# Draining GpSimd's indirect transfers in pairs, in a planned two-layer kernel on one core

## The chip, the core and the metric

The kernel runs on one core of one Trainium2 chip. A core has five engines that each work through a queue of their own in order: TensorE (PE) multiplies matrices, VectorE (DVE) and ScalarE (ACT) work on tiles element by element, GpSimd (POOL) does slower element work and issues transfers whose addresses come from data, and SyncE (SP) issues the other transfers. Semaphores order the queues among each other. The metric is the device time of one execution in microseconds; less is better.

## The reference

Eight sequences of 1024 tokens with 128 channels pass through two layers, each a mixer and a feed-forward network with a layer norm before it and a residual around it. Cut to what matters here:

```
x = L0_attn_x                                     # 8 x 1024 x 128
x = x + L0_attn(layernorm(x))                     # decayed linear attention, a scan over tokens
x = x + L0_ffn(layernorm(x))                      # 8 experts, top 2, hidden width 352
x = x + L1_attn(layernorm(x))                     # conv, gate, selective scan with 16 states
x = x + L1_ffn(layernorm(x))                      # 8 experts, top 2, width 128, and 2 shared ones

# a routed network, for each token:
scores = softmax(xn @ Wg.T); w, idx = top_k(scores, 2)
y = sum over e in idx of w_e * (silu(xn @ W1[e].T) * (xn @ W3[e].T)) @ W2[e].T
```

## The kernel before

Each sequence is one job of four stages, `l0_attn`, `l0_ffn`, `l1_attn` and `l1_ffn`, on tiles of 128 x 1024. The eight jobs overlap: at most five hold an x tile at once, and instructions of several stand mixed in each engine's queue.

The order of the work is fixed when the program is built. Every step is recorded with `op` (line 106): its engine, a planner's duration in us, what it reads and writes, and `land`, the time a transfer takes to land after its issue. `Schedule.run` (line 144) is a list scheduler. It keeps a clock for each engine, takes the step with the earliest start, and among steps that can start within `NEAR` of each other takes the one that is due first. `AHEAD` and `STAY` hold back ScalarE steps that would load another activation table. The due times come from `TIMES` (line 63), a row for each sequence: when its x is loaded, and for each of the four stages the due times of its first, second and last part. `START` (line 74) has the due times of the copies of the weights and of the zeroing of the scratch arrays. Nothing of this runs on the chip: there each engine takes its instructions in the order written, and waits on semaphores alone.

The two routed networks use scratch arrays in device memory. `dispatch` (line 767) normalizes x, routes, works out a row number `at` for each of 2 x 1024 token copies, so that each block of 128 rows belongs to one expert, copies the normalized rows on GpSimd (line 792) to add the second copy's weight, and then puts the rows into `xd` with sixteen indirect transfers of 128 rows from GpSimd (line 813). `block_pair` (line 844) loads two blocks of `xd` with SyncE into `xg` and transposes them on TensorE; `fetch` loads the block's expert weights; the result is weighted on ScalarE (line 879) and stored in `yd`. `combine` (line 825) gets the rows back with sixteen indirect transfers on GpSimd (line 832), eight for each of two tiles `g`, and after each eight adds the tile to x on GpSimd (line 842). The next stage's layer norm reads x on VectorE (line 478).

The last sequence's `l1_ffn` is computed densely, without routing, so there are 15 dispatches and 15 combines, with 240 puts and 240 gets.

GpSimd has one more task, in `l1_attn`: for each of the 16 states VectorE scans (line 1025) into one of four `st` tiles, multiplies it, and for all states but the first GpSimd adds the product to y (line 1035). These adds, the puts, the gets and the adds to x share GpSimd's queue.

Of the kernel before, what the change touches and what calls it, by code (L numbers as in the profile page):

```python
# [18 lines left out]
P = 128  # L19
T = 1024  # L20
NC = T // P
# [19 lines left out]
NST = 16  # L41
# [9 lines left out]

PE, DVE, ACT, POOL, SP = ENGINES = "PE", "DVE", "ACT", "POOL", "SP"
HOP = 0.1
NEAR = 0.141
TABLE = 1.3
AHEAD = 44.7
STAY = 675.97


FREE = "wide", "acc", "row", "tile64", "xg", "xgT", "h", "ysb"  # L60


TIMES = (
    (0.00, (266.32, 1847.59, 2307.10), (3760.69, 4450.59, 4867.29), (4934.72, 4936.07, 5074.67), (5113.40, 5139.16, 5310.29)),
    (3.56, (3273.27, 4241.54, 4793.32), (4824.85, 4945.95, 4955.40), (5096.98, 5279.14, 5301.11), (5442.87, 5510.48, 5668.30)),
    (28.59, (3893.45, 4841.22, 4949.32), (4949.33, 5011.59, 5200.87), (5345.49, 5546.91, 5863.91), (5880.85, 5880.86, 6091.76)),
    (119.24, (4827.78, 4983.48, 5011.45), (5165.22, 5267.56, 5525.66), (5818.86, 6051.79, 6090.06), (6103.71, 6186.21, 6934.85)),
    (389.34, (5188.77, 5392.69, 5604.20), (5636.54, 5802.06, 6027.87), (6100.87, 6527.36, 6941.79), (7032.13, 7164.73, 7772.04)),
    (504.89, (5416.94, 5669.81, 5921.96), (5948.26, 6168.24, 6435.93), (6843.69, 7190.63, 7603.76), (7857.58, 7879.15, 8348.80)),
    (728.44, (6007.28, 6161.19, 6660.77), (6720.53, 6797.55, 7398.14), (7815.93, 8928.93, 9119.46), (9483.85, 9651.23, 10294.32)),  # L70
    (977.51, (6389.60, 6695.97, 7179.18), (7248.10, 7635.87, 7924.00), (8346.44, 9746.01, 10107.23), (10122.54, 10230.87, 10523.57)),
)

START = 65.94, 32.93, 130.54, -2689.22, 619.92, 9.07


class Buf:
# [133 lines left out]
def preln_two_layer_kernel(ctx: ExitStack, tc: tile.TileContext, a: dict, out: bass.AP):  # L211
    nc = tc.nc
# [149 lines left out]
    def pick(r):  # L362

        return eye3b[:, r : r + 1].to_broadcast([TERMS * NBC, P])
# [45 lines left out]
        return t.unsqueeze(2).to_broadcast([P, NC, n])  # L410

    def dve_us(n, two=True):
        return 0.1 + n * (1.04e-3 if two else 0.62e-3)

    def act_us(n):
        return 0.14 + n * 0.86e-3

    def tt(out_, in0, in1, alu, n, r, w, eng=DVE):
        e = nc.vector if eng == DVE else nc.gpsimd
        us = dve_us(n) if eng == DVE else 0.1 + n * 2.35e-3  # L420
        op(eng, us, lambda: e.tensor_tensor(out_(), in0(), in1(), alu), r, w)  # L421

    def stt(out_, in0, scalar, in1, op0, op1, n, r, w):
# [30 lines left out]
            hold=hold,  # L454
        )

    def mm_cols(dst, m, lhsT, rhs, r, us=1.0):


        def fn():  # L460
            for s in range(T // HALF):
                nc.tensor.matmul(  # L462
                    dst.f[:m, ts(s, HALF)], lhsT(), rhs()[:, ts(s, HALF)], start=True, stop=True
                )

        op(PE, 2 * us, fn, r, [dst])

    def normal(x):

        xw, stats = Buf("xw"), Buf("stats")  # L470
        total, dev, var = Buf("row"), Buf("row"), Buf("row")
        st = lambda i: stats.f.rearrange("p (c s) -> p c s", s=6)[:, :, i]
        row = lambda b: lambda: b.f


        def moments():
            for c in range(NC):
                nc.vector.bn_stats(stats.f[:, 6 * c : 6 * c + 6], x3(x)[:, c, :])  # L478

        op(DVE, NC * 0.2, moments, [x], [stats])  # L480
        tt(row(dev), lambda: st(1), lambda: st(4), ALU.subtract, NC, [stats], [dev])
        tt(row(var), lambda: st(2), lambda: st(5), ALU.add, NC, [stats], [var])
        stt(row(dev), row(dev), 0.25, row(dev), ALU.mult, ALU.mult, NC, [dev], [dev])
        stt(row(var), row(var), 1.0 / P, row(dev), ALU.mult, ALU.add, NC, [var, dev], [var])

        act(row(var), row(var), AF.Ln, NC, [var], [var], "exp", bias=eps)
        tt(row(total), lambda: st(1), lambda: st(4), ALU.add, NC, [stats], [total])
        rstd, shift = Buf("row"), Buf("row")
        act(row(rstd), row(var), AF.Exp, NC, [var], [rstd], "exp", scale=-0.5)
        stt(row(shift), row(total), -0.5, row(rstd), ALU.mult, ALU.mult, NC, [total, rstd], [shift])  # L490

        def scale():
            for c in range(NC):
                nc.scalar.activation(  # L494
                    v3(xw, NC, XW)[:, c, :P], x3(x)[:, c, :], AF.Identity,
                    scale=rstd.f[:, c : c + 1], bias=shift.f[:, c : c + 1],
                )

        op(ACT, NC * 0.26, scale, [x, rstd, shift], [xw])
        return xw  # L500

    def turned(xw, tag):

        pt, xnT = Buf("wide"), Buf(tag)

        def fn():
            for c in range(NC):
                nc.tensor.transpose(pt.f[:, ts(c, P)], v3(xw, NC, XW)[:, c, :P], ident)

        op(PE, 1.6, fn, [xw], [pt])  # L510
        copy_act(lambda: xnT.f, lambda: pt.f, T, [pt], [xnT])
        return xnT

    def router(xnT, wgT, bias):
# [9 lines left out]
                    v3(pg, NC, NE)[:, c, :], xnT.f[:, ts(c, P)], wgT, start=True, stop=True  # L524
                )

        op(PE, 1.9, logits, [xnT], [pg])
        mx, p, tot = Buf("row"), Buf("tile64"), Buf("row")
        reduce(lambda: mx.f, t3(pg), ALU.max, n, [pg], [mx])
        tt(t3(p), t3(pg), lambda: per_token(mx.f, NE), ALU.subtract, n, [pg, mx], [p])  # L530
# [108 lines left out]
    def to_tokens(parts, consume, r=()):  # L639

        for q in range(NC // 4):
            po = Buf("acc")

            def fn(po=po, q=q):
                for i in range(4):
                    for j, (h, w) in enumerate(parts):
                        nc.tensor.matmul(  # L647
                            v3(po, 4, P)[:, i, :],
                            h.f[:, ts(4 * q + i, P)],
                            w(),  # L650
                            start=(j == 0),
                            stop=(j == len(parts) - 1),
                        )

            op(PE, 4 * len(parts) * 0.26, fn, [*(h for h, _ in parts), *r], [po])
            consume(4 * q, po)

    def add_to(x):
# [63 lines left out]
    def l0_attn(x, b):  # L722
# [23 lines left out]
        for f0 in range(0, EDIM, FGRP):  # L746
            parts = []
            for f in range(f0, f0 + FGRP):
                kv = Buf("kv")
                load(  # L750
                    lambda kv=kv: kv.f,
                    lambda f=f: heads_to_channels(vr.f[:, f, :]), 512, [vr], [kv],
                )
                tt(lambda kv=kv: kv.f, lambda: kT.f, lambda kv=kv: kv.f, ALU.mult, T, [kT, kv], [kv])
                op(
                    DVE, 2.25,
                    lambda kv=kv: nc.vector.tensor_tensor_scan(  # L757
                        kv.f, lam.f, kv.f, 0.0, ALU.mult, ALU.add
                    ),
                    [lam, kv], [kv],  # L760
                )
                tt(lambda kv=kv: kv.f, lambda: qT.f, lambda kv=kv: kv.f, ALU.mult, T, [qT, kv], [kv])
                parts.append((kv, lambda f=f: o_rep[:, f, :]))
                yield
            to_tokens(parts, add_to(x))

    def dispatch(x, i, tag, wgT, bias):
# [40 lines left out]
        views = dram_disjoint_views(xd[i], TOPK * NC)  # L808
        for k in range(TOPK):
            for c in range(NC):  # L810
                op(
                    POOL, 1.3,
                    lambda k=k, c=c: nc.gpsimd.indirect_dma_start(  # L813
                        out=views[k * NC + c],
                        out_offset=bass.IndirectOffsetOnAxis(
                            ap=v3(at, TOPK, NC)[:, k, c : c + 1].bitcast(I32), axis=0
                        ),
                        in_=r3[k]()[:, c, :],
                        in_offset=None,
                    ),  # L820
                    [rows[k], at], [(xd_b[i], (k, c))], land=2.8,
                )
        return at, expert, xnT

    def combine(x, i, at):

        for k in range(TOPK):
            g = Buf("tmp")
            for c in range(NC):
                op(  # L830
                    POOL, 1.28,
                    lambda k=k, c=c, g=g: nc.gpsimd.indirect_dma_start(  # L832
                        out=v3(g, NC, P)[:, c, :],
                        out_offset=None,
                        in_=yd[i],
                        in_offset=bass.IndirectOffsetOnAxis(
                            ap=v3(at, TOPK, NC)[:, k, c : c + 1].bitcast(I32), axis=0
                        ),
                    ),
                    [yd_b[i], at], [(g, c)], land=2.5,  # L840
                )
            tt(lambda: x3(x), lambda: x3(x), lambda g=g: v3(g, NC, P), ALU.add, T, [x, g], [x], POOL)

    def block_pair(i, xdb):
# [10 lines left out]
            for q in range(n):  # L855
                nc.tensor.transpose(pt.f[:, ts(q, P)], v3(xg, 2, XW)[:, q, :P], ident)

        op(PE, 0.05 + 0.18 * n, turn, [xg], [pt])
        copy_act(lambda: xgT.f[:, : n * P], lambda: pt.f[:, : n * P], n * P, [pt], [xgT])
        return n, xg, xgT, ysb  # L860

# [30 lines left out]
    def l0_ffn(x, b):  # L892
# [4 lines left out]
        def second(i, we, h, xg, ysb):  # L897
# [8 lines left out]
                        start=(j == 0), stop=(j == 2),  # L906
                    )

            op(PE, 0.85, fn, [h, we], [py])
            weigh(py, xg, ysb, i, 0)  # L910
            if i % 2 or i == NBLK - 1:
                keep(ysb, ydb, i - i % 2, i % 2 + 1)
# [2 lines left out]
        for i in range(NBLK):  # L915
# [11 lines left out]
                            start=True, stop=True,  # L927
                        )

            op(PE, 1.6, first, [we, xgT], [p13])  # L930
            act(lambda h=h: h.f, lambda p13=p13: p13.f[:, : 3 * P], AF.Silu, 3 * P, [p13], [h], "silu")
            tt(
                lambda h=h: h.f, lambda h=h: h.f, lambda p13=p13: p13.f[:, HALF : HALF + 3 * P],
# [11 lines left out]
    def l1_attn(x, b):  # L945
# [67 lines left out]
        for n in range(NST):  # L1013
# [1 line left out]
            act(  # L1015
                lambda da=da: da.f, dtf, AF.Exp, T, [dt], [da], "exp", scale=a_mat[:, n : n + 1]
            )
            mm_cols(pb, P, lambda n=n: pick(n), b3, [bc3], us=0.3)
            tt(
                lambda pb=pb: pb.f, lambda: dtx.f, lambda pb=pb: pb.f, ALU.mult, T,  # L1020
                [dtx, pb], [pb],
            )
            op(
                DVE, 2.25,
                lambda st=st, da=da, pb=pb: nc.vector.tensor_tensor_scan(  # L1025
                    st.f, da.f, pb.f, 0.0, ALU.mult, ALU.add
                ),
                [da, pb], [st],
            )
            mm_cols(pcc, P, lambda n=n: pick(NST + n), b3, [bc3], us=0.3)  # L1030
            stf = lambda st=st: st.f
            hc, hcf = (st, stf) if n else (y, yf)
            tt(hcf, stf, lambda pcc=pcc: pcc.f, ALU.mult, T, [st, pcc], [hc])
# [48 lines left out]
    def l1_ffn(x, b):  # L1082
# [22 lines left out]
        def second(i, n, w, h, xg, ysb):  # L1105
# [6 lines left out]
                        start=True, stop=True,  # L1112
                    )

            op(PE, 0.38 * n, fn, [h, *w], [py])
            for q in range(n):
                weigh(py, xg, ysb, i + q, q * P)
            keep(ysb, ydb, i, n)
# [2 lines left out]
        for i in range(0, NBLK, 2):  # L1121
# [9 lines left out]
                            start=True, stop=True,  # L1131
                        )

            op(PE, 0.7 * n, first, [xgT, *w], [p13])
            hf = lambda h=h, n=n: h.f[:, : n * P]
            act(hf, lambda p13=p13, n=n: p13.f[:, : n * P], AF.Silu, n * P, [p13], [h], "silu")
            tt(
# [108 lines left out]
```

## Time and profile before

| | |
|---|---|
| median of 3 runs | 2038.16 us (2036.46 to 2038.98) |
| the profiled execution | 2030.27 us |
| its span, first to last instruction | 2028.5 us |
| instructions in the span | 24,884 |
| mean granted TensorE clock | 0.819 of full |
| indirect transfers on GpSimd | 480, 31.61 MB on the software queue |
| transfers issued by SyncE | 247.81 MB on queue q1 |
| activation table loads on ScalarE | 198, 1.283 us each |

The profiled execution is one execution with the hardware profiler on; its own time is 7.9 us under the median of the three timed runs. The span lies 1.8 us under its time. Shares of busy time are averages over the span. An instruction of GpSimd that issues a transfer is shown as DMA_INDIRECT with the time that GpSimd spent on it; the transfer itself is seen in the packets of the software queue.

### The profile page before, as it was taken

To read this page: it belongs to the slowest core of one execution; us is meant where nothing else is said; L and a number is where in the kernel's file an instruction comes from. 1 tells how busy PE (TensorE), PEld (TensorE's weight loads), DVE (VectorE), ACT (ScalarE), POOL (GpSimd) and SP (SyncE) were. 2 spreads that over 40 slices of the span, in tenths; PEclk is the share of its full clock that TensorE was granted. 3 is DMA by queue.
4 is the path that set the end of the run, shared out by engine and by line. 5 is a ranking of instruction groups with operands and counts; after the bars stand their busy time and mean duration, and the time that the engine had idled before them with its cause. 6 is when DMAs were issued, how large, how long until landed. Compare 5 with 4: busy or idle time off the path is not lost. (4 is left out here: it accounts for less than half of the span.)

```text
span 2028.5 us, 24884 instructions
## 1 busy us (share of the span) xinstructions
PE 1385.9 (68%) x7693; PEld 1062.5 (52%) x7693; DVE 1441.4 (71%) x2117; ACT 998.4 (49%) x1657; POOL 895.1 (44%) x662
## 2 busy tenths in 40 slices
PE   2448786867666778567856676956765767656587
PEld 0336775646453665455654565645754555433365
DVE  1775656877566978499865977799756626888955
ACT  3213332753745575345746456663744366583441
POOL 0030312255346632666354574276455633736613
PEclk9759797888977889768887888977886788786679
DMA  5847575344336465444435664634543555332231
GB/s 131 199 123 201 178 215 152 113 147 150 115 106 186 120 182 163 105 139 130 131 121 154 188 180 126 192 106 140 166 143 116 160 160 166 84 99 63 75 89 56
DMA packets 215740, 282.54 MB, mean 139 GB/s; under 512 B 24248, under 2 KB 173112, under 8 KB 215608
## 3 DMA queue, kind: packets, MB, share of 16 engines
q1 hardware_dynamic: 194504, 247.81, 42.2%
q0 software_dynamic: 15360, 31.61, 5.2%
q10 hardware_dynamic: 5744, 1.54, 0.4%
q8 instruction: 61, 1.00, 0.2%
q14 instruction: 71, 0.58, 0.1%
HBM read 223.62 MB, written 63.15 MB: 141 GB/s over the span
## 5 line engine op out<-in xcount | busy, mean ns | idle before, releaser
L421 POOL TENSOR_TENSOR y<-y,st 128x1024 f32<-128x1024 f32 x120 | 291.7, 2430 | 299.1 <-DVE st L421 284.2
L925 PE MATMUL wide<-xgT,we 128*128 128x128 f32 x2208 | 323.9, 305 | 56.1 <-ACT xgT L449 15.2
L832 POOL DMA_INDIRECT tmp<-yd,at x240 | 260.8, 1087 | 216.8 <-issue 93.6
L925 PEld LDWEIGHTS wide<-xgT,we 128*128 128x128 f32 x2208 | 305.1, 219 | 82.6 <-ACT xgT L449 19.1
L1025 DVE TENSOR_TENSOR_SCAN st<-da,wide 128x1024 f32<-128x1024 f32 x128 | 292.4, 2284 | 8.2
L462 PE MATMUL wide<-term,eye3b 96*128 96x512 bf16 x512 | 178.3, 448 | 131.6 <-DVE st L1025 83.2
L904 PE MATMUL acc<-we,h 128*128 128x128 f32 x1104 | 182.9, 309 | 122.8 <-DVE h L421 63.7
L393 ACT ACT_TABLE_LOAD x198 | 254.0, 1283 | 18.0 <-DMA wgT<-in_gate_wT_dram 14.5
L904 PEld LDWEIGHTS acc<-we,h 128*128 128x128 f32 x1104 | 159.5, 216 | 154.6 <-issue 57.0
L813 POOL DMA_INDIRECT xd<-xw,at x120 | 123.9, 1033 | 247.2 <-DVE at L634 183.4
L879 ACT ACTIVATE ysb<-acc,xg 128x128 f32<-128x128 f32 x345 | 115.9, 363 | 218.2 <-PE acc L904 65.5
L421 DVE TENSOR_TENSOR h<-h,wide 128x384 f32<-128x384 f32 x184 | 99.7, 547 | 155.5 <-ACT h L446 103.1
L446 ACT ACTIVATE h<-wide 128x384 f32<-128x384 f32 x184 | 89.5, 489 | 242.7 <-PE wide L925 176.5
L421 DVE TENSOR_TENSOR wide<-dtx,wide 128x1024 f32<-128x1024 f32 x128 | 156.6, 1224 | 60.0 <-PE wide L462 27.5
L446 ACT ACTIVATE da<-dt,a_mat 128x1024 f32<-128x1024 f32 x128 | 145.8, 1147 | 101.7 <-DVE st L1025 73.6
L647 PE MATMUL acc<-o_rep,kv 128*128 128x128 f32 x1024 | 140.8, 301 | 47.7 <-DVE kv L421 43.3
L647 PEld LDWEIGHTS acc<-o_rep,kv 128*128 128x128 f32 x1024 | 135.7, 215 | 54.1 <-DVE kv L421 46.1
L421 DVE TENSOR_TENSOR st<-st,wide 128x1024 f32<-128x1024 f32 x120 | 146.1, 1218 | 24.1 <-remote 14.8
L757 DVE TENSOR_TENSOR_SCAN kv<-lam,kv 128x1024 f32<-128x1024 f32 x64 | 154.3, 2411 | 1.4
L792 POOL COPY tmp<-xw 128x1024 f32<-128x1024 f32 x15 | 18.6, 1242 | 297.5 <-ACT xw L494 214.5
L462 PEld LDWEIGHTS <-eye3b 96*128 96x128 bf16 x512 | 56.5, 111 | 176.6 <-issue 163.7
L813 POOL DMA_INDIRECT xd<-tmp,at x120 | 126.5, 1054 | 36.6 <-issue 36.3
(149 smaller groups left out, 2306.3 us busy)
## 6 DMA issues: line engine op xcount, KB each, us to landing
we<-w_rows SPq DMA_DIRECT2D x184, 544.0 KB
kv<-v_rows SPq DMA_DIRECT2D x64, 512.0 KB
fe<-f_rows SPq DMA_DIRECT2D x169, 192.0 KB
xg<-xd SPq DMA_DIRECT2D x165, 129.0 KB
yd<-ysb SPq DMA_DIRECT2D x165, 128.0 KB
xd<-zrow SPq DMA_DIRECT2D x4, 1483.5 KB
x<-in_x_dram SPq DMA_DIRECT2D x8, 512.0 KB
v_rows<-tmp SPq DMA_DIRECT2D x8, 512.0 KB
```

What stands on the lines that cost most here:

```text
L393: nc.scalar.add_instruction(mybir.InstLoadActFuncSet(name=nc.get_next_instruction_name(), act_func_set_id=tables[table], ins=[], outs=[]))
L421: op(eng, us, lambda: e.tensor_tensor(out_(), in0(), in1(), alu), r, w)
L446: op(ACT, act_us(n), lambda: nc.scalar.activation(out_(), in_(), func, **kw), r, w, table)
L462: nc.tensor.matmul(dst.f[:m, ts(s, HALF)], lhsT(), rhs()[:, ts(s, HALF)], start=True, stop=True)
L647: nc.tensor.matmul(v3(po, 4, P)[:, i, :], h.f[:, ts(4 * q + i, P)], w(), start=(j == 0), stop=(j == len(parts) - 1),)
L757: lambda kv=kv: nc.vector.tensor_tensor_scan(kv.f, lam.f, kv.f, 0.0, ALU.mult, ALU.add),
L813: lambda k=k, c=c: nc.gpsimd.indirect_dma_start(out=views[k * NC + c], out_offset=bass.IndirectOffsetOnAxis(ap=v3(at, TOPK, NC)[:, k, c : ...
L832: lambda k=k, c=c, g=g: nc.gpsimd.indirect_dma_start(out=v3(g, NC, P)[:, c, :], out_offset=None, in_=yd[i], in_offset=bass.IndirectOffsetO ...
L879: lambda: nc.scalar.activation(v3(ysb, 2, P)[:, i % 2, :], py.f[:, c0 : c0 + P], AF.Copy, scale=v3(xg, 2, XW)[:, i % 2, P : P + 1],),
L904: nc.tensor.matmul(py.f[:, :P], v3(h, 3, P)[:, j, :], we.f[:, c0 : c0 + P], start=(j == 0), stop=(j == 2),)
L925: nc.tensor.matmul(p4[:, m, j, :], we.f[:, c0 : c0 + P], xgT.f[:, ts(i % 2, P)], start=True, stop=True,)
L1025: lambda st=st, da=da, pb=pb: nc.vector.tensor_tensor_scan(st.f, da.f, pb.f, 0.0, ALU.mult, ALU.add),
```

## The change

After every second put and every second get GpSimd executes a drain. The planner's durations are changed for many steps: the second transfer of a pair is planned with 3.5 us (puts) or 3.3 us (gets) on GpSimd and 0.6 us to land, where each transfer had 1.3 or 1.28 us, and 2.8 or 2.5 us to land; the durations of other engines' steps become longer, by 2 to 50%. The due times in `TIMES` and `START` and the constants `NEAR`, `AHEAD` and `STAY` are other ones. What each step computes, the tiles and their number are the same.

```diff
-NEAR = 0.141
+NEAR = 0.110
 TABLE = 1.3
-AHEAD = 44.7
-STAY = 675.97
+AHEAD = 63.9
+STAY = 582.37
...
 TIMES = (
-    (0.00, (266.32, 1847.59, 2307.10), (3760.69, 4450.59, 4867.29), (4934.72, 4936.07, 5074.67), (5113.40, 5139.16, 5310.29)),
+    (0.00, (1956.55, 3364.95, 4337.94), (4437.11, 4795.86, 5832.50), (6047.30, 6138.90, 6283.74), (6328.36, 6345.19, 6499.52)),
...
-START = 65.94, 32.93, 130.54, -2689.22, 619.92, 9.07
+START = -2927.59, 76.99, 43.57, 480.48, 574.17, 99.43
...
     def dve_us(n, two=True):
-        return 0.1 + n * (1.04e-3 if two else 0.62e-3)
+        return 0.15 + n * (1.05e-3 if two else 0.55e-3)
 
     def act_us(n):
-        return 0.14 + n * 0.86e-3
+        return 0.25 + n * 0.86e-3 if n < 100 else 0.24 + n * 0.86e-3
...
-        op(ACT, NC * 0.26, scale, [x, rstd, shift], [xw])
+        op(ACT, NC * 0.4, scale, [x, rstd, shift], [xw])
...
-                op(
-                    POOL, 1.3,
-                    lambda k=k, c=c: nc.gpsimd.indirect_dma_start(
+                def put(k=k, c=c):
+                    nc.gpsimd.indirect_dma_start(
                         out=views[k * NC + c],
...
-                    ),
-                    [rows[k], at], [(xd_b[i], (k, c))], land=2.8,
+                    )
+                    if c % 2:
+                        nc.gpsimd.drain()
+
+                op(
+                    POOL, 3.5 if c % 2 else 1.3, put, [rows[k], at], [(xd_b[i], (k, c))],
+                    land=0.6 if c % 2 else 2.8,
                 )
...
-                op(
-                    POOL, 1.28,
-                    lambda k=k, c=c, g=g: nc.gpsimd.indirect_dma_start(
+                def get(k=k, c=c, g=g):
+                    nc.gpsimd.indirect_dma_start(
                         out=v3(g, NC, P)[:, c, :],
...
-                    ),
-                    [yd_b[i], at], [(g, c)], land=2.5,
+                    )
+                    if c % 2:
+                        nc.gpsimd.drain()
+
+                op(
+                    POOL, 3.3 if c % 2 else 1.3, get, [yd_b[i], at], [(g, c)],
+                    land=0.6 if c % 2 else 2.5,
                 )
...
-            op(PE, 4 * len(parts) * 0.26, fn, [*(h for h, _ in parts), *r], [po])
+            op(PE, 4 * len(parts) * 0.28, fn, [*(h for h, _ in parts), *r], [po])
...
-            op(PE, 1.6, first, [we, xgT], [p13])
+            op(PE, 1.78, first, [we, xgT], [p13])
```

## The prediction

> **What bounds it now.** I read the busy shares first, then the costliest groups, the waits on GpSimd, the end of GpSimd's timeline, the chain that ended last, and the stages.
>
> ```profile
> PE 1385.9 (68%) x7693; PEld 1062.5 (52%) x7693; DVE 1441.4 (71%) x2117; ACT 998.4 (49%) x1657; POOL 895.1 (44%) x662
> ...
> L421 POOL TENSOR_TENSOR y<-y,st 128x1024 f32<-128x1024 f32 x120 | 291.7, 2430 | 299.1 <-DVE st L421 284.2
> ...
> L832 POOL DMA_INDIRECT tmp<-yd,at x240 | 260.8, 1087 | 216.8 <-issue 93.6
> ...
> L813 POOL DMA_INDIRECT xd<-xw,at x120 | 123.9, 1033 | 247.2 <-DVE at L634 183.4
> ```
>
> No engine is full. DVE leads with 71%, so 587 of its 2028.5 us are idle: the span is set by how eight chains of stages interleave on in-order queues. GpSimd is the emptiest engine but one row matters: its adds to y (2.43 us each) and its 480 indirect transfers (about 1 us each) share one queue.
>
> ```profile
> ACT xw L494 <- DMA xd<-xw,at: 20.1, 4, 14.2
> POOL x L421 <- DMA tmp<-yd,at: 8.7, 4, 3.1
> DVE stats L478 <- POOL x L421: 7.7, 1, 7.7
> ...
> DVE y L421 <- POOL y L421: 2.2, 1, 2.2
> ```
>
> These are the rows of the waits in which someone waited for GpSimd or its transfers (total us, times, longest); SyncE's own list adds 8.1 us for the puts and 6.8 us for the adds to x. Together under 60 us in the whole span: the timetable keeps GpSimd ahead of its readers.
>
> ```profile
> 1741.92 0.98 POOL L832 DMA_INDIRECT tmp<-yd,at  x1
> 1743.20 0.95 POOL L832 DMA_INDIRECT tmp<-yd,at  x1 [0.30 <-issue]
> ...
> 1770.93 2.34 POOL L421 TENSOR_TENSOR x<-x,tmp 128x1024 f32<-128x1024 f32 x1
> ...
> 1885.53 0.97 POOL L813 DMA_INDIRECT xd<-tmp,at  x1 [0.30 <-issue]
> 1886.52 9.62 POOL L421 TENSOR_TENSOR y<-y,st 128x1024 f32<-128x1024 f32 x4
> ```
>
> GpSimd's timeline (start, us): the last sequence's first combine runs 1741.9 to 1773.3, and the first read of its x on DVE starts only 2.7 us later. The sixteen puts of 1866.4 to 1886.5 leave four adds to y standing behind them, as many as there are st buffers.
>
> ```profile
> 1888.66 2.30 DVE st L1025
> 1894.51 2.29 DVE st L1025
> 1897.98 2.27 DVE st L1025
> ```
>
> The chain that ended last passes through the scans of that last sequence, some 5 us apart, and then its dense FFN. So near the end GpSimd's spare time is small.
>
> ```profile
> 800.00:1100.00 300.00, 196.42 (x1143) 157.69 (x1142) 224.37 (x342) 143.50 (x243) 165.34 (x123) 0.80 0.44 129
> 1100.00:1400.00 300.00, 222.10 (x1271) 170.25 (x1270) 243.83 (x322) 174.79 (x295) 164.88 (x109) 0.85 0.54 159
> ```
>
> In the middle (columns PE, PEld, DVE, ACT, POOL) GpSimd is busy 165 of 300 us and DVE 224 to 244.
>
> **The drains.** 240 are added: eight for each of 15 dispatches and 15 combines. The number of puts, gets, adds and copies is unchanged. If a drain holds GpSimd until the pair has landed, its price is the flight of the second transfer after its instruction ended. The software queue shows 15,360 packets, 32 for each of 480 transfers; cutting their 4-byte closing packets by time into sixteens gives, from the instruction's end to the last packet, for puts (L813) a median of 1.2 us, mean 1.7, ninth decile 3.1; for gets (L832) 1.6, 2.2 and 4.7. I take the means, since a pair still meets the weights' traffic: 120 x 1.7 + 120 x 2.2 = 468 us more on GpSimd. With 895 us busy and about 0.3 us ahead of each of some 645 instructions (194 us) that makes 1557 us, 77% of the span: GpSimd goes from the emptiest to the most loaded. The ends are the smallest flights, 0.9 and 1.1 us (240 us), and the ninth deciles (936 us).
>
> The trace holds one drain that had work ahead of it:
>
> ```profile
> L1232 POOLq DRAIN  x1: 186/186/186, 0.3 to 0.3; - x1
> ```
>
> It waited for memsets, not transfers. At its length the 240 would be 45 us on GpSimd and nothing on the path, which I keep as a rival. On the other side a gain from fewer transfers under way is small: the software queue (q0) holds the DMA engines for 5.2% of the span, the weights' queue (q1) for 42.2%.
>
> The Trainium skill, "PSUM — Partial Sum Buffer", section Engine vs sequencer instructions, says a drain waits until the engine is fully idle, and "Perfetto Trace Analysis", section DMA Instruction — SWDGE (GPSIMD), says a transfer's instruction ends in the profile when its descriptors are written, not when its data has moved. Read together they speak against the change: the drain would end with the descriptors, and by that the sum would be that of the third rival instead of 22 us on the path. No run here shows which.
>
> What is late next. A dispatch's readers (SyncE's loads of xg) get the last rows 7 x 1.7 = 11.9 us later, the eighth drain being a landing they await anyway; a combine's readers 7 x 2.2 = 15.4 us later. The cover is the gap that stands there now. From the last put's end to the first load of xg the 15 gaps are 1.5 (twice), 6.9, 11.1, 13.6, 14.1 (twice), 18 and more (eight); less 1.7 us of flight, four of them fall short of 11.9: by about 12, 12, 7 and 2.5. From the last add to x to the next layer's DVE statistics the gaps are 0.0, 2.7, 4.3, 12.5, 14.1 and 16.6 or more (three): short of 15.4 by 15, 13, 11, 3 and 1. In all 76 us, at nine places over eight overlapping sequences, so only what lies on the last chain counts in full. There, two places:
> - The last sequence's first combine: 15.4 us, its cover of 2.7 us left for other small lateness. Its later start is open to the new order, so this is the larger end; the lower is 0.
> - The sixteen puts ahead of the last sequence's adds to y. GpSimd is held 8 x 1.7 = 13.6 us longer, and in the new order all fifteen adds of that sequence stand behind those puts, where two stood ahead before. DVE can run four scans ahead, at 5 us some 20 us, and those four are already in use. Cost 0 to 13.6; I take half, 6.8.
>
> Sum of the drains: 15.4 + 6.8 = 22 us.
>
> **Durations and timetable.** They add no work; they reorder nearly everything. Table loads go from 198 to 200: 2 x 1.28 = 2.6 us on an ACT that is half idle, nothing. The new planner durations are nearer to the rows: 0.24 + 1024 x 0.86e-3 = 1.12 us for an exponential that takes 1.147 (before 1.02), 0.35 for a 128-column scaling that takes 0.363 (0.25), 1.225 for a DVE product that takes 1.218 to 1.224 (1.165). What a truer plan is worth no row shows. Bounds: DVE's idle time is 587 us, of which 130.4 ended with ACT's h and 74.3 with issue, head-of-queue time that a better order can shrink; a tenth of 587 is 59 us of gain. On the other side a plan that must place 468 us more on GpSimd can spend the whole 76 us of shortfalls where it paid 22: 54 us of loss. The stages stand where they stood: the work of each sequence and layer begins and ends within three points or so of DVE's instruction time. So I take a small gain, 6 us, a tenth of its end. The scheduled NEAR, AHEAD, STAY and START act only through this order.
>
> Sum: 2030.3 (the profiled execution; 2028.5 of it span) + 22 - 6 = 2046.3. The median of the runs is 2038.16, 7.9 above the profiled one, so 2054.
>
> **Rivals.**
> 1. *The new order wins.* For it: 587 us of DVE idle, planner durations that were 10 to 30% short on ACT, nearly no waits on GpSimd that drains could lengthen outside the last chain. Against: the unchanged shape of the stages. Price: 59 us of the idle won, 22 paid: 2038 - 37 = 2001. It is on the other side; it decides once the reordering gives over 22 us, 4% of DVE's idle.
> 2. *GpSimd becomes the bound.* In the windows of 800 to 1400, 165 busy plus a seventh of 468 in each 300 us (69) plus gaps of about 30 is 264 of 300, above DVE. At the ninth deciles it is 165 + 138 + 30 = 333 of 300: over by 33 in each of two stages, and with the 22 at the end 2038 + 88 = 2126. For it: the y adds behind pairs, and the fixed order in which one late transfer holds all. Against: means that leave a tenth free, and less crowding with two transfers out. It decides from a flight of about 3 us.
> 3. *The drain does not hold until landing.* 45 us on GpSimd, hidden, and the 6 us of reordering, but a plan made for longer transfers: 2038 - 6 = 2032, within 0 to 12 us of gain. For it: the one drain of the trace is short. Against: that drain had no transfer ahead of it; the change's own planner costs (3.5 and 3.3 us for the second of a pair, against 1.3) are a plan, not a measurement. It decides if a drain takes some 0.3 us or less.
>
> **Chances.** The forecast, 0.2 to 2.6% slower: 0.45. Rival 1: 0.29. Rival 2: 0.12. Rival 3: 0.08, of which 0.05 faster. What is left, 0.06, is drains and order cancelling. A measurement of this kernel can tell about 0.2% (4 us) from no change, so: faster 0.29 + 0.05 = 0.34; the same 0.03 + 0.06 = 0.09; slower 0.57. The likeliest case's own range is 2042 to 2092, from 4 us, where the plan's gain nearly cancels the drains, to 54 us, where the plan pays the whole 76 in place of 22. The range that holds 8 in 10 reaches into rivals 1 and 2: 1990 to 2105.
>
> **What would show it.** Drains on GpSimd's sequencer with a mean of 1.5 to 2.5 us (rival 3: under 0.3). Pairs of DMA_INDIRECT 1.3 us apart, then a pause of 2 us; a dispatch that spans 34 us and a combine 37 or more. GpSimd's busy row still near 895 us, as the drains are not counted, but "DVE waits for POOL" and "SyncE waits for the puts" over 100 us in all. The last sequence's scans with gaps over 5 us behind the last puts. DVE's busy time unchanged within 1%. I am wrong if DVE's idle falls while drains hold (rival 1), or if DVE waits long for y in the middle stages (rival 2).

## The result and the profile after

| kernel | median us | runs |
|---|---|---|
| before | 2038.57 | 2036.46 to 2044.35, four runs |
| after | 2192.22 | 2187.66 to 2199.71, four runs |

The ratio is 1.075, interval 1.0721 to 1.0778: 7.5% slower, where 0.8% slower was forecast and 3.3% was the upper end of the range. The profiled execution of after took 2191.13 us, 2189.4 of it span, at a mean granted clock of 0.805 (before: 0.819).

One thing is needed to read the tables below: kernels are compared only within one session (several kernels run one after another on one chip), since in some sessions the kernel before takes about 2036 us in nearly all its runs, and in others about 1865 (called here the 2036 sessions and the 1865 sessions). The comparison above is of the first sort.

The busy row and the costliest groups of after (line, engine, operation, tiles, count; then busy us, mean ns; then idle time of the engine before them and what ended most of it):

```profile
PE 1419.9 (65%) x7693; PEld 1083.6 (49%) x7693; DVE 1451.1 (66%) x2117; ACT 1006.2 (46%) x1659; POOL 893.7 (41%) x662
...
L835 POOL DMA_INDIRECT tmp<-yd,at x240 | 262.1, 1092 | 416.9 <-issue 329.9
L1033 DVE TENSOR_TENSOR_SCAN st<-da,wide 128x1024 f32<-128x1024 f32 x128 | 292.5, 2285 | 137.5 <-POOL y L421 129.8
L421 POOL TENSOR_TENSOR y<-y,st 128x1024 f32<-128x1024 f32 x120 | 287.9, 2399 | 120.8 <-DVE st L421 68.4
...
L812 POOL DMA_INDIRECT xd<-xw,at x120 | 130.8, 1090 | 303.0 <-issue 197.3
```

The work is what it was: DVE is busy for 0.7% longer, GpSimd for 1.4 us less. All of the loss is idle time. The idle time ahead of the gets rose from 216.8 to 416.9 us, 329.9 of it "issue", which is how the page shows a drain: GpSimd waits for nothing that has a row. And the largest idle time ahead of the y adds has turned round. Before, GpSimd waited 284.2 us for DVE's products; now that is 68.4, and DVE's scans wait 129.8 us for GpSimd.

The drains themselves stand on GpSimd's sequencer (count, then shortest, median and longest in ns; first is that of the puts, second that of the gets):

```profile
L821 POOLq DRAIN  x120: 3401/4168/14395, 153.1 to 2047.8; - x120
L844 POOLq DRAIN  x120: 2781/4880/11729, 313.2 to 2163.0; - x120
```

Such a record begins while the pair's own instructions still run. From the end of the pair's second instruction to the end of the drain it is 2.50 us in the mean for puts (median 1.86) and 2.68 for gets (1.97), 621 us in all. The 3.55 us for gets in an expectation below takes the wrong get for the pair's second one: in many combines a get of the second tile stands among those of the first, so that not every second get in the queue is a pair's second.

GpSimd's timeline at the end of the last dispatch, and behind it:

```profile
2042.99 0.97 POOL L812 DMA_INDIRECT xd<-tmp,at  x1 [2.19 <-issue]
2044.26 0.97 POOL L812 DMA_INDIRECT xd<-tmp,at  x1 [0.30 <-issue]
2047.55 0.97 POOL L812 DMA_INDIRECT xd<-tmp,at  x1 [2.31 <-issue]
2048.82 0.97 POOL L812 DMA_INDIRECT xd<-tmp,at  x1 [0.31 <-issue]
2051.34 16.91 POOL L421 TENSOR_TENSOR y<-y,st 128x1024 f32<-128x1024 f32 x7 [1.55 <-issue]
```

and SyncE's and DVE's at the same place:

```profile
2051.22 1.92 SPq L453 DMA_DIRECT2D xg<-xd  x4
```

```profile
2037.08 2.29 DVE L1033 TENSOR_TENSOR_SCAN st<-da,wide 128x1024 f32<-128x1024 f32 x1
2053.70 2.29 DVE L1033 TENSOR_TENSOR_SCAN st<-da,wide 128x1024 f32<-128x1024 f32 x1 [10.69 <-POOL y L421]
```

Pairs 1.27 us apart and a pause after each: that is the drain. Two readers stand right behind the last put. SyncE issues its loads of xg 1.4 us after it, with no spare time left. And the last sequence's adds to y begin only behind the puts, seven in a row, while DVE, out of st buffers, stands for 10.69 us. In 11 of after's 15 dispatches the first load of xg follows the last put by 1.4 to 1.6 us; before it was 2 of 15.

The waits on GpSimd (total us, times, longest), of ACT and DVE and then of SyncE's queue:

```profile
DVE st L1033 <- POOL y L421: 129.8, 15, 22.9
...
DVE stats L478 <- POOL x L421: 38.4, 2, 23.5
...
ACT xw L494 <- DMA xd<-xw,at: 31.6, 16, 3.5
...
DVE y L421 <- POOL y L421: 27.2, 3, 15.8
```

```profile
SPq L453 <- DMA xd<-tmp,at: 105.1, 33, 26.3
...
SPq L453 <- POOL x L421: 67.1, 6, 17.6
```

About 400 us, where before had under 60. The same two windows as before (columns of busy us: PE, PEld, DVE, ACT, POOL; then clock and DMA):

```profile
800.00:1100.00 300.00, 202.67 (x1088) 156.23 (x1086) 229.84 (x328) 160.04 (x250) 140.90 (x97) 0.80 0.41 119
1100.00:1400.00 300.00, 204.75 (x1153) 163.10 (x1154) 213.44 (x294) 149.54 (x248) 139.13 (x97) 0.82 0.49 144
```

DVE does 5 us more work in the first and 30 us less in the second. GpSimd gets through 97 instructions in each, where it was 123 and 109, and is busy for 25 us less: it is held, not loaded.

### The profile page after: what moved, and what is told of

It reads as the page before. It is cut to its first block, busy times and chain, and to the rows that moved or that the text cites. A ratio compares the mean times of both kernels' runs of the same rounds, so it can differ in the third digit from the quotient of the medians.

```text
span 2189.4 us, 25221 instructions
## 1 busy us (share of the span) xinstructions
PE 1419.9 (65%) x7693; PEld 1083.6 (49%) x7693; DVE 1451.1 (66%) x2117; ACT 1006.2 (46%) x1659; POOL 893.7 (41%) x662
## 5 line engine op out<-in xcount | busy, mean ns | idle before, releaser
L835 POOL DMA_INDIRECT tmp<-yd,at x240 | 262.1, 1092 | 416.9 <-issue 329.9
L933 PE MATMUL wide<-xgT,we 128*128 128x128 f32 x2208 | 338.7, 315 | 133.3 <-DVE st L1033 60.6
L933 PEld LDWEIGHTS wide<-xgT,we 128*128 128x128 f32 x2208 | 316.2, 226 | 164.8 <-DVE st L1033 54.3
L1033 DVE TENSOR_TENSOR_SCAN st<-da,wide 128x1024 f32<-128x1024 f32 x128 | 292.5, 2285 | 137.5 <-POOL y L421 129.8
L421 POOL TENSOR_TENSOR y<-y,st 128x1024 f32<-128x1024 f32 x120 | 287.9, 2399 | 120.8 <-DVE st L421 68.4
L462 PE MATMUL wide<-term,eye3b 96*128 96x512 bf16 x512 | 183.2, 458 | 156.7 <-DVE st L1033 122.1
L812 POOL DMA_INDIRECT xd<-xw,at x120 | 130.8, 1090 | 303.0 <-issue 197.3
L912 PE MATMUL acc<-we,h 128*128 128x128 f32 x1104 | 175.0, 301 | 67.2 <-DVE h L421 40.8
L912 PEld LDWEIGHTS acc<-we,h 128*128 128x128 f32 x1104 | 154.3, 210 | 96.0 <-DVE h L421 41.3
L508 PE MATMUL wide<-ident,xw 128*128 128x128 f32 x256 | 55.1, 330 | 131.1 <-ACT xw L494 122.3
```

The source lines that it names most:

```text
L462: nc.tensor.matmul(dst.f[:m, ts(s, HALF)], lhsT(), rhs()[:, ts(s, HALF)], start=True, stop=True)
L812: nc.gpsimd.indirect_dma_start(out=views[k * NC + c], out_offset=bass.IndirectOffsetOnAxis(ap=v3(at, TOPK, NC)[:, k, c : c + 1].bitcast(I3 ...
L835: nc.gpsimd.indirect_dma_start(out=v3(g, NC, P)[:, c, :], out_offset=None, in_=yd[i], in_offset=bass.IndirectOffsetOnAxis(ap=v3(at, TOPK, ...
L912: nc.tensor.matmul(py.f[:, :P], v3(h, 3, P)[:, j, :], we.f[:, c0 : c0 + P], start=(j == 0), stop=(j == 2),)
L933: nc.tensor.matmul(p4[:, m, j, :], we.f[:, c0 : c0 + P], xgT.f[:, ts(i % 2, P)], start=True, stop=True,)
L1033: lambda st=st, da=da, pb=pb: nc.vector.tensor_tensor_scan(st.f, da.f, pb.f, 0.0, ALU.mult, ALU.add),
```

## The experiments

Two parts were taken apart: the drains, and the order (planner durations, TIMES, NEAR, AHEAD, STAY, START). Not every duration in it grows by 2 to 50%: one of ScalarE's goes from 0.26 to 0.4, and a few shrink, GpSimd's adds from 2.51 to 2.46 us. "Order of before" means that the instructions stand on every queue as they do in before, with the drains put in between.

**First session: each part alone.** Drains only; order of before:

```diff
-                op(POOL, 1.3, lambda k=k, c=c: nc.gpsimd.indirect_dma_start(...), ..., land=2.8)
+                def put(k=k, c=c):
+                    nc.gpsimd.indirect_dma_start(...)
+                    if c % 2:
+                        nc.gpsimd.drain()
+                op(POOL, 1.3, put, ..., land=2.8)
```

(the same for the gets, with 1.28 and 2.5).

> The kernel before with the 240 drains and nothing else: the order of every queue is that of before. Theory A (the drains themselves set the loss: each holds GpSimd about 3 us beyond its pair and makes the readers of dispatch and combine late): 2140 us or more, SyncE's and DVE's waits on GpSimd's work over 200 us in all. Theory B (the order made for long transfers is the loss, the drains cost what was forecast): 2045 to 2080. Theory C (the new order softens the drains): above the 2192 of the changed kernel.

The changed order alone, all else as after:

```diff
                     )
-                    if c % 2:
-                        nc.gpsimd.drain()
```

(twice, in put and in get).

> The changed kernel without its 240 drains: its durations, due times and the order of every queue stay. Theory A: 2000 to 2070, close to the kernel before. Theory B: 2120 or more. Under C it lies below 2192 by less than e1 lies above 2038.

Drains on the puts only, and on the gets only, in the order of before (one half of the first edit each):

> The kernel before with the 120 drains of the dispatches alone. If the late puts are the main loss (SyncE's loads of xg wait for them): more than half of e1's loss. If the loss goes by the time held (2.5 us against 3.55 for a get's pair): about 0.4 of it.

> The kernel before with the 120 drains of the combines alone. By the time held about 0.6 of e1's loss; if the two losses are on one chain, e3 and e4 add up to e1, and if each hides the other, they add up to more.

| kernel | us | ratio to before, 1867.61 | loss, us |
|---|---|---|---|
| drains only | 2323.07 | 1.2451 (1.241 to 1.2492) | 455 |
| new order only | 1958.81 | 1.0487 (1.0454 to 1.052) | 91 |
| drains on puts | 2104.38 | 1.1277 (1.1227 to 1.1327) | 237 |
| drains on gets | 2104.45 | 1.1278 (1.1244 to 1.1312) | 237 |

Two things follow. The drains cost the old order twenty times the 22 us that I gave them, and the two halves add up (474 against 455): the lateness of the puts does not cover that of the gets. The holds of this kernel, measured as in after and with the restart that is worked out in the part on the prediction, are some 660 us, so about two thirds of them are paid. And the new order by itself is no gain but a loss. The session also showed before at 1867.61 us, which no theory of mine had: the first of the 1865 sessions.

**Second session: before and after again, and two changes of one size.**

> The kernel before, unchanged, to have its profile from the chip of the experiments, where it takes 1868 us against 2038 in the first comparison. Theory F (in the first comparison the other engines stood still at times while GpSimd's indirect transfers ran, with no releaser that the profile names, and here they do not): 1855 to 1880 us, waits put down to 'remote' or 'issue' on DVE and ACT under 40 us in all against some 400 there. Otherwise those waits are here too and the difference lies elsewhere, such as in the granted clock.

> The changed kernel, unchanged. Theory F with drains that end those standstills: it takes about as long as in the first comparison, 2150 to 2200, so its ratio here is 1.15 to 1.18 and not 1.075. If the chips differ in speed alone: ratio 1.075, some 2005 us.

A drain after each fourth transfer, in the order of before (120 drains in place of 240):

```diff
+                    if c % 4 == 3:
+                        nc.gpsimd.drain()
```

> As e1 (order of before), with a drain after each fourth transfer, so 120 drains and four transfers under way at most. If the loss goes by the number of drains: half of e1's 455 us, 2080 to 2110. If the landing of the last transfer of a group, once for each dispatch and combine, makes most of the loss: above 2200.

The new order without drains, planned with the transfer costs of before:

```diff
-                    POOL, 3.5 if c % 2 else 1.3, put, [rows[k], at], [(xd_b[i], (k, c))],
-                    land=0.6 if c % 2 else 2.8,
+                    POOL, 1.3, put, [rows[k], at], [(xd_b[i], (k, c))],
+                    land=2.8,
```

(for the gets 1.28 and 2.5).

> As e2 (no drains, new due times and new durations of the other engines), but the planner takes the transfers at the costs of before (1.3 and 1.28 us, landing after 2.8 and 2.5). If planning for long transfers made e2 4.9% slower than before: within 2% of before. If the due times themselves are worse, or fit only the long transfers: 4% slower or more.

| kernel | us | ratio to before, 2036.43 |
|---|---|---|
| before | 2034.65 | 0.9983 (0.9945 to 1.002) |
| after | 2192.0 | 1.0754 (1.0687 to 1.0822) |
| old order, drains by fours | 2050.24 | 1.0076 (1.0043 to 1.0109) |
| new order, short transfer costs | 2131.36 | 1.0446 (1.0379 to 1.0514) |

With half the drains the loss is 14 us. That is not to be set against the first session's 455, as this one is of the 2036 sort; there the drains in pairs cost 283 (fifth session). The long planned transfers (3.5 and 3.3 us) are not what makes the new order slow: planned short it is 95 us slower than before all the same.

**Third session**, on the question whether the first one's 1867 comes again, with the drains by fours in the new order and by eights in the old:

> e1 again (order of before, drains in pairs), since the chips so far are of two kinds: on one the kernel before takes 1868 us and shows no standstills, on the other it takes 2036 and shows them. On a chip of the second kind, Theory F (drains in pairs end the standstills, so what is left is the order and the holds, alike on both): 2300 to 2340, ratio 1.13 to 1.15. If the standstills stay under drains: 2450 or more. On a chip of the first kind 2323 again.

> e2 again (the changed kernel without drains). On a chip of the second kind, where nothing holds back the transfers: Theory F has the standstills come back and adds some 170 us to the 1959 of the other chip, 2100 to 2160, so that the drains of the changed kernel cost only 40 to 90 us there. If the standstills belong to the order of before: 1960 to 2000.

```diff
+                    if c == NC - 1:
+                        nc.gpsimd.drain()
```

> The order of before with a drain after each eighth transfer, 60 in all, eight transfers under way at most. By the number of drains a quarter of e1's loss on a chip without standstills, some 115 us: 1980 there. On a chip with them: if eight under way are few enough to end them, about 1980 as well, 2 to 3% faster than before; if they need four or fewer, 2050 or more, with 'remote' waits on ACT and DVE over 100 us.

> The changed kernel with a drain after each fourth transfer in place of each second, its plan unchanged. By the number of drains half of what they cost it: on a chip without standstills 1959 plus some 110, about 2070; on one with them the same if four under way are few enough, as e7's missing 'remote' waits say, which is 5% faster than the changed kernel and still slower than before.

| kernel | us | ratio to before, 1863.48 |
|---|---|---|
| drains only | 2314.03 | 1.2413 (1.2363 to 1.2463) |
| new order only | 1954.2 | 1.0487 (1.0469 to 1.0504) |
| old order, drains by eights | 1925.43 | 1.0347 (1.03 to 1.0394) |
| new order, drains by fours | 2020.31 | 1.0841 (1.0822 to 1.0859) |

A second 1865 session, on another chip, with the results of the first.

**Fourth session: the same kernels in a 2036 session.**

> The changed kernel, unchanged. Theory F (its drains leave no standstills, so both kinds of chip run it alike): 2170 to 2200 on either; on a chip where before takes 1865 the ratio is then 1.165 to 1.18. If part of its loss on the first chip was standstills: 2080 or less where before takes 1865.

> The order of before with a drain after each fourth transfer. Theory F: 2040 to 2060 as on chip 12, also where before takes 1865. If four under way still leave standstills on chip 12: 1990 or less where before takes 1865.

> The changed kernel without drains. Where before takes 2036, Theory F: 2100 to 2160, with 'remote' and 'issue' waits of over 300 us on DVE, ACT and PE, so that the drains cost the changed kernel some 60 us there. If the standstills belong to the order of before: 1960 to 2000. Where before takes 1865: 1956 again.

> The order of before with a drain after each eighth transfer. Where before takes 2036: if eight under way are few enough to end the standstills, 1920 to 1940 and 5% faster than before; if not, 2050 or more with 'remote' waits over 100 us. Where before takes 1865: 1925 again.

| kernel | us | ratio to before, 2042.26 |
|---|---|---|
| after | 2204.95 | 1.0798 (1.0748 to 1.0848) |
| old order, drains by fours | 2059.52 | 1.0088 (1.0053 to 1.0122) |
| new order only | 2122.44 | 1.0393 (1.0344 to 1.0443) |
| old order, drains by eights | 1991.53 | 0.9764 (0.972 to 0.9808) |

**Fifth session**, with after and the drains alone in one session:

> The changed kernel, unchanged. Where before takes 1865: Theory F 2170 to 2210, ratio 1.16 to 1.185, so drains in pairs cost the changed order some 230 us there against 82 where there are standstills. If the chip is slower beside the standstills too: 2080 to 2150. Where before takes 2036: 2190 to 2205 again.

> The order of before with drains in pairs. Where before takes 2036: Theory F 2310 to 2350, ratio 1.13 to 1.15, and so the changed order saves some 120 us of the drains' loss while it costs 80 without them. If the standstills stay under drains in pairs: 2450 or more. Where before takes 1865: 2318 again.

| kernel | us | ratio to before, 2032.62 |
|---|---|---|
| after | 2196.57 | 1.0815 (1.0772 to 1.0858) |
| drains only | 2315.23 | 1.1408 (1.1347 to 1.147) |

It was a 2036 session, on the chip that had the first session. Some of the expectations above speak of two kinds of chip; the fifth session refutes that. The kind belongs to the session, and what sets it stays open.

**What sets the two kinds of session apart.** The new order without drains is the same program in both, 2122.44 us in the fourth session and about 1956 in the first and third. Its busy rows in the first session and then in the fourth:

```profile
PE 1393.2 (71%) x7693; PEld 1063.4 (54%) x7693; DVE 1474.1 (75%) x2117; ACT 1003.7 (51%) x1659; POOL 904.4 (46%) x662
```

```profile
PE 1442.8 (68%) x7693; PEld 1099.2 (52%) x7693; DVE 1468.5 (69%) x2117; ACT 1005.2 (47%) x1659; POOL 897.9 (42%) x662
```

DVE, ACT and GpSimd are busy as long within 1%. PE is 50 us longer, with a granted clock of 0.803 against 0.835, in a span that is 163 us longer; how much of the 163 us PE's clock makes was not taken apart. The rest shows in the waits. The fourth session's execution has these rows:

```profile
ACT h L446 <- remote: 76.0, 12, 14.0
...
ACT ysb L883 <- remote: 45.0, 7, 10.2
...
DVE x L421 <- remote: 32.4, 3, 15.8
```

The first session's execution has no row with "remote" at all. The profile before has them too:

```profile
ACT h L446 <- remote: 90.6, 16, 10.2
...
DVE h L421 <- issue: 74.3, 17, 13.4
...
DVE x L421 <- remote: 39.9, 7, 11.4
...
ACT ysb L879 <- remote: 34.4, 9, 6.0
```

What such a row is shows in the timeline of before, of PE, ACT, DVE and then GpSimd around the same ten microseconds (PE's first row has the matmuls whose results the two rows of ACT read):

```profile
841.74 2.05 PE L1129 MATMUL acc<-xgT,fe 128*128 128x128 f32 x16
...
849.44 1.22 PE L1110 MATMUL acc<-fe,h 128*128 128x128 f32 x4 [5.21 <-issue]
...
860.00 0.69 PE L856 MATMUL acc<-ident,xg 128*128 128x128 f32 x2 [9.33 <-issue]
```

```profile
848.55 0.38 ACT L446 ACTIVATE h<-acc 128x256 f32<-128x256 f32 x1 [3.69 <-issue]
859.10 0.38 ACT L446 ACTIVATE h<-acc 128x256 f32<-128x256 f32 x1 [10.17 <-remote]
```

```profile
848.97 0.42 DVE L421 TENSOR_TENSOR h<-h,acc 128x256 f32<-128x256 f32 x1 [3.56 <-issue]
859.52 0.42 DVE L421 TENSOR_TENSOR h<-h,acc 128x256 f32<-128x256 f32 x1 [10.13 <-issue]
```

```profile
850.43 0.94 POOL L832 DMA_INDIRECT tmp<-yd,at  x1 [0.30 <-issue]
...
856.73 0.94 POOL L832 DMA_INDIRECT tmp<-yd,at  x1 [0.30 <-issue]
```

Three engines stand still together for 8.4 us, while GpSimd goes on with a get each 1.25 us until 857.67. ACT's wait is for PE: the matmuls that it reads at 859.10 ended at 843.79 by the profile. The trace also records each step of a semaphore (the signal by which one engine releases another), and what ends this wait is a step of PE's semaphore at 859.08, 8.4 us after the end of PE's last matmul before it. DVE stands behind ACT and PE behind DVE, and these pass the signal on within 0.1 us. So it is in all 45 "remote" waits of before and in the 149 of the other profiles: the step is PE's, recorded 1.5 to 12.3 us after the end of its last matmul. "remote" says here that the signal came late, not that another core was waited for.

In before there are 28 stretches of over 1.5 us in which PE, DVE and ACT are all idle, 129 us; in 23 of them GpSimd was issuing indirect transfers. In the first session's execution of the new order there are 8 (53 us), five of them in the first 100 us, and one with indirect transfers. Idleness of all three is not the sign by itself: after has 29 such stretches, 209 us, and no "remote" wait.

With drains the "remote" waits go. Their sum over ACT and DVE in the 2036 sessions is 226 us in before (231 in its repeat), 170 in the new order alone and 245 with that order planned short, 103 with drains by eights, 1.4 and 0 by fours, 0 in after (in all four profiles) and in the drains only. In the 1865 sessions none of the eight profiles has one; before was not profiled there. Waits of ACT, DVE and PE put down to "issue" fall less far in the 2036 sessions: 273 us in before, 103 and 107 by fours, 67 to 87 in after and 47 in the drains only, against 5 to 13 in the 1865 profiles. So it is not shown that nothing is left by fours.

The traces of the two kinds of session differ in one more thing. In the eight 1865 profiles nearly every step of a semaphore is on record: of the 21,808 that the landings of transfers make, 21,739 to 21,786. In the twelve 2036 profiles many are missing: 13,904 to 14,110 are there without drains, 14,999 with drains by eights, 17,479 by fours, 19,308 to 19,473 in pairs. Of ACT's, DVE's and GpSimd's own steps some 310 are missing in before, all of them within 6 us of the start of an indirect transfer. So late signals and lost records come together: both may have one cause, or the recording itself may make the signals late. Every execution here has its span and clock on record, so no run tells whether the standstills are there without the recording.

The waits of the old order with drains by eights, and then by fours, in the fourth session:

```profile
ACT h L446 <- remote: 35.7, 9, 6.5
...
DVE x L421 <- remote: 15.6, 3, 6.6
```

```profile
DVE st L1033 <- POOL y L421: 122.2, 11, 20.9
...
ACT ysb L887 <- remote: 1.4, 1, 1.4
```

By eights "remote" waits are left and GpSimd is little late (the scans wait 38.9 us for y); by fours they are gone, but the scans' wait has grown to 122 us.

**What the drains alone do**, in the fifth session (waits of DVE and ACT, then SyncE's):

```profile
DVE st L1033 <- POOL y L421: 226.7, 13, 28.8
...
ACT xw L494 <- DMA xd<-xw,at: 75.2, 29, 13.9
...
ACT tmp L446 <- POOL x L421: 73.6, 5, 22.2
```

```profile
SPq L453 <- DMA xd<-tmp,at: 167.4, 34, 27.4
...
SPq L453 <- POOL x L421: 124.5, 7, 31.6
```

With the smaller rows the waits on GpSimd add up to about 767 us, against some 400 in after. The new order, slower without drains, makes room for them: with drains it is the faster one, 2197 us against 2315.

**The sum.**

| | 2036 sessions | 1865 sessions |
|---|---|---|
| before | 2033 to 2042 | 1863, 1868 |
| new order only | 2122 (+80) | 1954, 1959 (+91) |
| drains only | 2315 (+283) | 2314, 2323 (+451, +455) |
| both (after) | 2192 to 2205 (+154 to +164) | not run |

What the 2036 sessions add is about 170 us for before (2036 less 1865) and 166 for the new order (2122 less 1956), and next to nothing for the drains in pairs, 2315 against 2314 and 2323. That the added time is the standstills' is argued from the rows above; the difference in PE's clock is in it too. If after gains nothing in an 1865 session either, as its rows suggest, its loss is made up of: the order 91, the drains' holds in that order 2197 - 1956 = 241, the standstills ended -170, together 162. These three add up to the measured 154 to 164 by construction, since the 241 is taken from after itself, so they are an account and not a test. That after would take about 2197 us in an 1865 session is argued from this and was not run.

Of all versions run the drain after each eighth transfer in the order of before is the only one under the kernel before: 2.4% faster (1.9 to 2.8%) in a 2036 session, 3.5% slower in an 1865 session.

## Why the prediction was wrong, step by step

**What held.** The sign; that a drain holds GpSimd until the pair has landed; the pairs and pauses; the busy times of GpSimd (893.7, forecast near 895) and DVE; waits on GpSimd of over 100 us. Rival 3 falls: the drains' rows have medians of 4.2 and 4.9 us, not 0.186. The Trainium skill, "PSUM — Partial Sum Buffer", section Engine vs sequencer instructions, has a drain wait until the engine is idle. Here it waited longer than for GpSimd's instructions: it ended, by the median, 0.56 us (puts) and 0.46 us (gets) after the pair's last packet, and never before it, and over the 240 drains the hold follows the flight with a correlation of 0.99. So the reading of the skill's two pages in the forecast, by which the drain ends with the descriptors, does not hold in this trace.

**The price of a drain** was mis-sized. I took the flight of the second transfer, 1.7 and 2.2 us, as the hold. In after that flight is 1.84 and 2.14 us, so the flight was right; but the drain ends 0.65 and 0.54 us (means) after the last packet, and the next instruction starts 0.71 us (median) after the drain's end, where 0.30 lies between two instructions without one. The forecast had nothing for these two. So the hold is 621 + 240 x 0.41 = 719 us, not 468. From first to last transfer a dispatch takes 42.8 us (forecast 34; before 21.5), a combine 48.5 (37; before 26.6).

**"Only what lies on the last chain counts in full"** is the step that failed most. I took the gaps ahead of the readers as covers, found 76 us short at nine places, and counted 22. The drains alone, in the very order that those gaps were read from, cost 283 us in the 2036 sessions and 453 in the others. In after each of the 15 dispatches and 15 combines is some 21 to 22 us longer, about 86 us for a sequence with two of each, and eight sequences share queues with a fixed order. A reader that is late holds SyncE's queue or DVE for all the other sequences, and the next dispatch then begins late itself. A gap that stands in one execution is not spare time of that place; it may be the only room that others had. In the 1865 sessions 455 of some 660 us of holds reached the span, where I had let 22 of 468 through. The rows show the lateness (SyncE's 167.4 us for the puts, the scans' 226.7 for y); that a late reader passes it on to other sequences in this way is argued, not measured place by place.

**"So I take a small gain, 6 us"** for durations and timetable: the sign failed. Alone they cost 80 us in a 2036 session and 91 in the 1865 sessions; planned with the transfer costs of before, 95 in a 2036 session. They do help with drains: after is 118 us under the drains only (2315 less 2197). Which of the due times, NEAR, AHEAD or durations does what was not taken apart.

**"A gain from fewer transfers under way is small"** failed, and its evidence was on the page. I measured it by the share of the DMA engines (q0, 5.2%), which says nothing of engines that stand still. The rows "remote" and "issue" of ACT, DVE and PE came to 499 us in before, against 67 in after, and I quoted 74.3 of them as room for a better order. The "remote" ones end with a late step of PE's semaphore, and GpSimd was issuing transfers in 23 of 28 common standstills. A gain of some 170 us, by the account above, was there in the executions of this comparison. It hid about half of the 332 us that the drains and the order cost by that account; without it my forecast would have missed by far more than 138 us.

Rival 1 (the order wins) is refuted by the order alone. Rival 2 comes nearest: GpSimd became the engine that others wait for, in the middle stages too, at a hold of 2.9 to 3.1 us each with the restart, at its point of "about 3 us". But its 2126 us, worked out as an excess of load in two stages, is 66 us short: the loss comes from lateness in every dispatch, not from GpSimd's load, which with its holds is 893.7 + 719 of 2189 us, 74%, still not full.

**Open:** why PE's signal comes late, and ACT and DVE with it, while indirect transfers are under way (that the transfers hold something on its way is argued, not shown, and so is that the recording has a part in it); what makes this appear in some sessions and not in others; what after takes in an 1865 session; and why the new order without drains is 4 to 5% slower.

## What to carry to other kernels

A wait put into an in-order queue can cost its length at each reader that the plan left no room, and a gap in a finished timetable is no proof of room: try the wait alone, in the old order, before setting the timetable anew. Idle time that no row ends ("remote", or "issue" on several engines at once) is not slack for a scheduler: look for what another engine is doing in just these stretches, for the last matmuls that should have ended them, and for whether the trace has all its records there. To limit transfers under way, begin with the loosest limit; here one drain for each eight was worth 51 us where standstills were present, one for each two cost 283.

## What the runs showed of the hardware

A drain on GpSimd waits for the indirect transfers issued ahead of it: in every one of after's 240 pairs it ended after the last packet, by 0.56 us for puts and 0.46 us for gets in the median (by eights 0.74 to 0.88); 0.71 us pass from there to the next instruction.

The same program takes 2122 us in one session and 1956 in others, at the same busy times of DVE, ACT and GpSimd. In the longer executions ACT and DVE wait up to 14.5 us for steps of PE's semaphore that come 1.5 to 12.3 us after its last matmul ended, mostly while GpSimd issues indirect transfers, and the trace loses semaphore records there. With a drain after each fourth transfer these "remote" waits are all but gone, with one after each eighth less than half of them is left (103 of 226 us).
